# A decoder layer on one core: z transposed by VectorE in blocks through DRAM from batch 4 on, first loads on ScalarE's queue, first expert's inner weights in four loads

## The chip, the core and the metric

One core of a Trainium2 chip. Its engines run side by side and wait for each other by semaphores: PE (TensorE, matrix products; PEld is its loading of weights), DVE (VectorE), ACT (ScalarE), POOL (GpSimd) and SP (SyncE). Transfers between DRAM and SBUF are issued by SP and by ACT, each on its own queue, and run on 16 DMA engines. The metric is the device time of one execution in microseconds, as the median of several executions.

## What is computed

The layer takes x (16 batches of 512 tokens, 256 features), a context (16 x 64 x 256) and a mask. Cut to what matters:

```python
# 1. linear self-attention, K = 2, 16 heads of 16
q  = x + x @ Wq + bq
ks = x + x @ Wk[k] + bk[k];  vs = x + x @ Wv[k] + bv[k]      # both scaled by 1/sqrt(1024)
state = prod_k(ks_k^T @ vs_k)                                # per head 16 x 16
out = q @ state                                              # "z" in the kernel
out = layernorm(out) * ln_g + ln_b
x = layernorm(x + out @ Wo + bo)
# 2. cross-attention to the context, 16 heads of 64
sim = (x @ xWq.T) @ (context @ Wkv.T)_k^T * 64 ** -0.5;  masked softmax
x = layernorm(x + (attn @ v) @ Wout.T + b_out)
# 3. mixture of 8 experts, capacity 1024 of the 8192 tokens for each
w = softmax(x @ router_w.T + router_b)
y_e = relu(tokens_e @ experts_inter[e]) @ experts_out[e] * w
x = layernorm(x + scatter_add(y_e))
```

All in float32. With these inputs every token has a positive weight for every expert, so the first 1024 tokens (batches 0 and 1, the "head") are those that go through the experts.

## The kernel before

Tokens of a batch lie on 128 partitions, four tiles of 128 (`NT`), features along the row; two halves of 128 features (`NC`) make the contraction. A matmul needs its operand with features on partitions, so each activation that is multiplied is also made in a transposed copy: `xT` (for `ps_o`, L775), `zT` (for `ps_p`, L799), `x1T` (for `ps_sim`, L933). Eight more columns (`E`, hence `CX` = 264) carry the router's scores along with x, z and x1.

The work of a batch runs in streams, written as Python generators: `all_grams` (gram matrices of x, L634 to L651), `all_self_attention` (L697: `g_times_wk`, `states`, z in L775, its norm, `zT`, then `ps_p` in L799), `scores_operand` (L807: x1, its norm and `x1T`), `all_cross_attention` (L876: `ps_sim`, softmax, `ps_x` in L954), `all_routing` (L966) and `experts` (L1060: `ps_h` in L1077, `ps_e` in L1094, all on batches 0 and 1). `weave` (L1141) picks the next stream by a plan of start and span, and by a `Model` (L28) of each engine's and transfer's duration, which holds a stream back until what it waits for should be there (`until(made(...))`). `in_order` (L1161) then fixes the order that came out for PE, DVE, ACT (with its DMA issues) and POOL. SP's issues stand in the order that the tile framework gives them. So a number in `Model`, as the 5.0 us of a transfer on ACT's queue (L87), moves the order of instructions; it is no time of the chip.

There are two ways to a transposed copy. The helper `transposed` (L243) uses PE: eight transposes into two PSUM banks, copied out by ACT or DVE. From batch 4 (`FIRST`) on, `xT` and `x1T` go in blocks: `to_blocks` (L268) has DVE transpose 32 x 32 blocks into `xb` (one buffer, guarded by `taken`), `put_blocks` (L283) writes `xb` to DRAM on ACT's queue, and `from_blocks` (L291) reads it back in four transfers on ACT's queue, each to 32 partitions, which sets the blocks in place. This trip changes the order of the tokens: where a tile takes it, the tokens come out as (block, place in block) exchanged. So `x1T`'s trip needs x1 in one order and leaves another, and the gram's x of batches 4 on is loaded with its rows in the exchanged order (L364), for `xT` to come out in the natural one. z is transposed by PE in every batch (L788): eight transposes `ps_zt`, and two ACT activations that apply gain and shift while they copy out of PSUM (L789).

Setup: the first loads are all issued by SP, in this order: x of batch 0 in four pieces (L359), the first 512 rows of the context and of Wkv (L490, L500), the second ones, x of batch 1, the key weights (L388 on). ACT's first instruction is the load of its function table (L218). The x that self-attention adds to (`xt`, `load_x`, L692) is loaded when z's batch begins. The first expert's inner weights (`load_inter`, L1109, 1 MB in one transfer) can only be loaded once the setup's buffers are given back (`setup.close`, L975), which is after batch 0's last norm; `experts` waits in the model for them (L1069).

Of the kernel before, what the change touches and what calls it, by code (L numbers as in the profile page):

```python
# [9 lines left out]
FP = mybir.dt.float32  # L10
I32 = mybir.dt.int32
U8 = mybir.dt.uint8
AF = mybir.ActivationFunctionType
# [5 lines left out]
P = 128  # L19
# [8 lines left out]
class Model:  # L28
# [37 lines left out]
    def run(self):  # L66

        traced = self.nc.cur_bb.bb.instructions
        now = self.free.get("PE", 0.0)
        end = max(self.end, now)  # L70
        for ins in traced[self.seen:]:
            kind, engine = type(ins).__name__, str(ins.engine).split(".")[-1]
            aps = [[a.bass_ap for a in l if hasattr(a, "bass_ap")] for l in (ins.ins, ins.outs)]
            names = [[a.name for a in l] for l in aps]
            at = 0.0
            for made, used, l in ((1, 0, names[0]), (1, 1, names[1])):
                for n in l:
                    if kind == "InstDMACopy" and self.made.get(n, (0, 0))[1] == "SP":
                        continue
                    for known, book in ((made, self.made), (used, self.used)):  # L80
                        if known and n in book:
                            t, by = book[n]
                            at = max(at, t + (self.WIDE.get(by, 0.0) if by != engine else 0.0))
            if kind == "InstDMACopy" and engine == "Activation":
                start = max(at, self.free.get(engine, 0.0))
                self.free[engine] = start + 0.35
                done = start + 5.0  # L87
            elif kind == "InstDMACopy":
                size = 4 * min(a.size() for l in aps for a in l)
                if now < 40:  # L90
                    issue = self.free["SP"] = max(at, self.free.get("SP", 0.8)) + 0.45
                    self.dma = max(issue + 1.2, self.dma) + size / 300e3
                    done = self.dma + 0.4
                else:
                    done = at + size / 220e3 + 2.0
            elif names[1]:
                start = max(at, self.free.get(engine, 0.0))
                done = self.free[engine] = start + self.duration(ins, kind, engine)
                if engine == "PE":
                    self.took += done - start  # L100
                else:
                    end = max(end, done + 0.15)
            else:
                continue
            for n in names[0] + names[1]:
                by = "SP" if kind == "InstDMACopy" else engine
                self.used[n] = max(self.used.get(n, (0.0, None)), (done, by), key=lambda p: p[0])
            for n in names[1]:
                self.made[n] = (done, "SP" if kind == "InstDMACopy" else engine)
        self.seen, self.end = len(traced), end  # L110
        return end
# [13 lines left out]
def decoder_layer(  # L125
# [60 lines left out]
    def bank(name):  # L186
        return psp.tile([P, 512], FP, tag="ps", name=name)
# [26 lines left out]
        return t  # L214

    nc.scalar.preload_act_table_set("natural_log_exp_and_others")  # L218
    ident = const.tile([P, P], FP, tag="ident", name="ident")
    make_identity(nc, ident)  # L220
    eps = const.tile([P, 1], FP, tag="eps", name="eps")
# [107 lines left out]
    with ExitStack() as att:  # L329
# [19 lines left out]

        def load_gram_x(b, eng=nc.sync):  # L350


            t = gp.tile([P, NT, C + 1], FP, tag="gx", name="gx")
            nc.gpsimd.memset(t[:, :, C:], 1.0)
            pieces = 1 if 0 < b < FIRST else NT
            n_ = NT // pieces
            for i in range(pieces):
                if b < FIRST:
                    eng.dma_start(  # L359
                        out=t[:, i * n_:(i + 1) * n_, :C],  # L360
                        in_=x[b, i * n_ * P:(i + 1) * n_ * P, :].rearrange("(t p) c -> p t c", p=P),
                    )
                else:
                    eng.dma_start(  # L364
                        out=t[i * 32:(i + 1) * 32, :, :C],
                        in_=x[b, i * P:(i + 1) * P, :].rearrange("(q j) c -> j q c", j=32),
                    )
            return t

        gram_x = {0: load_gram_x(0)}  # L370
# [114 lines left out]

        BJ = B * J

        def load_context(sp, q):
            t = wk2.tile([P, 4, C], FP, tag="vo", name="cn", bufs=6)
            nc.sync.dma_start(  # L490
                out=t,
                in_=context.rearrange("b j c -> (b j) c")[q * 512:(q + 1) * 512, :].rearrange(
                    "(i p) c -> p i c", p=P
                ),
            )
            return t

        def load_wkv(sp, r4):
            t = wk2.tile([P, 4, C], FP, tag="vo", name="nat", bufs=6)
            nc.sync.dma_start(out=t, in_=x_wkv[r4 * 512:(r4 + 1) * 512, :].rearrange("(r p) c -> p r c", p=P))  # L500
            return t

        NG = 512 // (GB * J)
# [183 lines left out]
                    sums[b // QB][1].append(key_sums(sums["u4"]))  # L687
                    yield WAIT

        grams, sums, x_blocks = {}, {}, {}  # L690

        def load_x(b):  # L692
            t = wk1.tile([P, NT, CX], FP, tag="xt", name="xt")
            nc.sync.dma_start(out=t[:, :, :C], in_=x[b].rearrange("(t p) c -> p t c", p=P))
            return t

        def self_attention(b, done):  # L697
# [47 lines left out]
            nc.vector.scalar_tensor_tensor(state, state, STATE_SCALE, headmask, ALU.mult, ALU.mult)  # L745

            yield from until(lambda: finished["x1"] >= b)
            xt = load_x(b)
            if b < FIRST:
                yield from until(lambda: made(xt))  # L750
                transposed(xT.rearrange("p t c n -> p c t n"), xt, lambda t: t)
# [29 lines left out]
            yield from normalized(z[:, :, :C], lambda t: z[:, t, :C], mm=mm)  # L781
            yield WAIT

            zT = wk1.tile([P, NC, S], FP, tag="xT", name="zT")
            for cc in range(NC):
                ps = bank("ps_zt")
                for t in range(NT):
                    nc.tensor.transpose(ps[:, t * P:(t + 1) * P], z[:, t, cc * P:(cc + 1) * P], ident)  # L788
                nc.scalar.activation(  # L789
                    zT[:, cc, :], ps, AF.Identity, bias=cs["shift"][:, cc:cc + 1], scale=cs["gain"][:, cc:cc + 1]  # L790
                )
            nc.gpsimd.tensor_copy(xt[:, :, C:], z[:, :, C:])
            nc.gpsimd.tensor_add(xt[:, :, :C], xt[:, :, :C], cs["bo"].unsqueeze(1).to_broadcast([P, NT, C]))
            yield WAIT
            mm = moments()
            for t in range(NT):
                ps = bank("ps_p")
                for cc in range(NC):
                    nc.tensor.matmul(  # L799
                        ps[:, :CX], zT[:, cc, t * P:(t + 1) * P], wo[:, cc, :], start=(cc == 0), stop=(cc == NC - 1)  # L800
                    )
                nc.vector.tensor_add(xt[:, t, :], ps[:, :CX], xt[:, t, :])
                moment(mm, t, xt[:, t, :])
                yield
# [161 lines left out]
        def routing(b, x1):  # L966
# [5 lines left out]
            if b == 0:  # L972

                yield from until(lambda: ("values", 1) in held)
                setup.close()  # L975
                ffn = pool(att, "ffn", 1)
                first_expert.extend((load_inter(0), load_outer(0)))
            if b < HEAD_B:
                head_T[b] = ffn.tile([P, NC, S], FP, tag=f"head_T{b}", name="head_T", bufs=1)
                transposed(head_T[b], x2)  # L980
# [79 lines left out]
        def experts():  # L1060
# [5 lines left out]
            for e in range(E):  # L1066
                if e == 0:
                    wi, wo_ = first_expert
                    yield from until(lambda: made(wi, wo_))  # L1069
                for n in range(CAP // TB):  # L1070
                    b, t0 = divmod(n * TB // P, NT)
                    yield from until(lambda: b in head_T and made(head_T[b]))
# [33 lines left out]
                    if n == CAP // TB - 1 and e + 1 < E:  # L1106
                        wo_ = load_outer(e + 1)

        def load_inter(e):  # L1109
            t = ffn.tile([P, NC, FF], FP, tag="wi", name="wi", bufs=1)  # L1110
            nc.sync.dma_start(out=t, in_=w_inter[e].rearrange("(c p) f -> p c f", p=P))
            return t

        def load_outer(e):
# [66 lines left out]
        def until(ready):  # L1181
            while not ready():
                yield 0.5

        def all_grams():
            for b in range(B):
                if b >= QB:
                    grams_st.plan(SETUP + (b - QB - 0.8) * STEP, STEP, 2.9)
                yield from until(lambda: finished["states"] > b - 5)
                yield from grams_of([b])  # L1190
                if b == 1:
                    yield from until(lambda: made(early, wk, nbk))
                    finish_key_weights()
                    yield from router_columns(rw)
                    yield
                if b == QB - 1:
                    cs.update(rest_of_weights(sp))
                    yield
                    yield from until(lambda: made(early, wo, wv))
                    finish_weights()  # L1200
                    yield WAIT
                    yield from router_weights(sp)
# [33 lines left out]

        setup = ExitStack()
        sp = pool(setup, "setup", 2)
        nats = [load(sp, q) for q in range(2) for load in (load_context, load_wkv)]
        gram_x[1] = load_gram_x(1)  # L1240
        key_weights()
        cs = {}
# [101 lines left out]
```

## Time and profile before

| | us |
|---|---|
| median of 3 runs (1355.06 to 1358.25) | 1355.67 |
| the profiled execution | 1358.28 |
| its span, first to last instruction | 1356.3 |
| PE busy | 1334.3 |
| DVE, ACT, POOL busy | 817.4, 422.5, 204.2 |
| mean granted TensorE clock | 0.996 |
| DMA engines, mean | 132 GB/s |

How to read the profile lines. A line of the timeline has the start and the length in us, the engine (a q behind it marks the engine's sequencer, as for an issued DMA), the source line, the operation, output<-input by the kernel's names, shape, how many, and in brackets the idle time of the engine just before it with what ended it. A line of the groups has, behind the bar, the busy time in us and the mean length of one in ns, then the idle time before them. A line of the waits reads "who <- what released it: us in total, times, longest". A line of the stretches has from:to, its length, then the busy time and number of instructions of PE, PEld, DVE, ACT and POOL, the mean granted clock of TensorE (1.00 is full), the share of the DMA engines in use and GB/s. "issue" is a wait that the profile puts down to nothing it shows. Matmuls overlap: the length of one (some 0.27 to 0.6 us) is a latency, and the pace is the distance from one to the next.

### The profile page before, as it was taken

What the parts mean: (1) busy time and instruction counts of PE and PEld (TensorE: products, weight loads), DVE (VectorE), ACT (ScalarE), POOL (GpSimd) and SP (SyncE); (2) the same over time, 40 slices, a digit from 0 to 9 for tenths busy, and PEclk for the clock granted to TensorE, in tenths of its full rate; (3) what the DMA queues carried; (4) which work ended last, traced back from release to release, by engine and by line L of the source; (5) the groups of instructions that cost most, each with busy time, mean ns of one, the idle gap of its engine ahead of it and who ended that gap; (6) DMA issues with size and microseconds to landing.
All of it is one profiled execution on the core that took longest, in us unless ns stands there. A gap on an engine that the chain in (4) does not pass through costs nothing.

```text
span 1356.3 us, 23928 instructions
## 1 busy us (share of the span) xinstructions
PE 1334.3 (98%) x9438; PEld 1052.6 (78%) x9438; DVE 817.4 (60%) x1961; ACT 422.5 (31%) x970; POOL 204.2 (15%) x140
## 2 busy tenths in 40 slices
PE   8999998999999999999999999999999999999997
PEld 5676675887788787887788787877788787878796
DVE  1265837556474747567555758566655848474844
ACT  2244424242222514143222414142323304142323
POOL 0010201112021111202021111202111112112100
PEclk9999998999999999999999999999999999999999
DMA  8737474421535353723645353623635153605411
GB/s 264 210 128 241 159 225 157 118 74 41 151 119 150 110 152 96 205 70 112 172 128 142 95 154 124 185 64 110 182 88 155 63 160 109 176 30 126 129 56 41
DMA packets 115204, 178.73 MB, mean 132 GB/s; under 512 B 17032, under 2 KB 83856, under 8 KB 115088
## 3 DMA queue, kind: packets, MB, share of 16 engines
q1 hardware_dynamic: 97808, 151.98, 39.1%
q10 hardware_dynamic: 17280, 25.17, 5.5%
q8 instruction: 76, 1.25, 0.4%
q14 instruction: 40, 0.33, 0.1%
HBM read 127.29 MB, written 49.81 MB: 131 GB/s over the span
## 4 chain that ended last, share of the span: by engine, by line
PE 93%; DVE 4%; DMA 1%; issue 1%; ACT 1%; SPq 0%; POOL 0%; POOLq 0%; DVEq 0%; ACTq 0%
PE ps_x L954 17%; PE ps_h L1077 16%; PE ps_sim L933 15%; PE ps_e L1094 15%; PE ps_p L799 4%; PE ps_o L775 4%; PE ps_kv L511 4%; PE ps_gk L712 4%; PE ps_vo L571 2%; PE ps_kq L862 2%; PE ps_s L724 2%; PE ps_g L634 2%; PE ps_m L757 1%; PE ps_zt L788 1%; PE ps_g L639 1%; PE ps_t L249 1%
## 5 line engine op out<-in xcount | busy, mean ns | idle before, releaser
L1077 PE MATMUL ps_h<-head_T,wi 128*128 128x256 f32 x1024 | 243.4, 383 | 4.0 <-issue 4.0
L933 PE MATMUL ps_sim<-kq,x1T 128*128 128x512 f32 x512 | 237.8, 593 | 0.0
L1077 PEld LDWEIGHTS ps_h<-head_T,wi 128*128 128x128 f32 x1024 | 194.2, 192 | 49.8 <-issue 20.9
L954 PE MATMUL ps_x<-vo,pT 32*128 32x264 f32 x4096 | 232.5, 383 | 0.2 <-DVE off L321 0.2
L954 PEld LDWEIGHTS ps_x<-vo,pT 32*128 32x128 f32 x4096 | 209.5, 185 | 20.8 <-issue 2.3
L920 POOL TENSOR_TENSOR s<-s,sm 128x1024 f32<-128x1024 f32 x64 | 121.7, 1901 | 650.2 <-DVE sm L919 572.5
L961 DVE TENSOR_TENSOR x<-ps_x,x 128x264 f32<-128x264 f32 x64 | 23.2, 425 | 234.9 <-PE ps_x L954 234.9
L1083 ACT ACTIVATE hT<-ps_h 128x256 f32<-128x256 f32 x177 | 67.7, 382 | 302.3 <-PE ps_h L1077 266.8
L933 PEld LDWEIGHTS ps_sim<-kq,x1T 128*128 128x128 f32 x512 | 96.2, 190 | 77.7 <-issue 69.8
L939 DVE TENSOR_REDUCE mx<-ps_sim 128x8 f32<-128x512 f32 x128 | 86.2, 674 | 59.4 <-PE ps_sim L933 58.6
L911 ACT ACTIVATE s<-s 128x512 f32<-128x512 f32 x128 | 79.3, 624 | 88.9 <-DVE s L940 68.9
L940 DVE TENSOR_TENSOR s<-ps_sim,mx 128x512 f32<-128x512 f32 x128 | 88.5, 692 | 4.4
L922 DVE STREAM_TRANSPOSE pT<-s 128x1024 f32<-128x1024 f32 x64 | 78.5, 1226 | 4.5 <-POOL s L920 4.2
L918 DVE TENSOR_REDUCE sm<-s 128x16 f32<-128x1024 f32 x64 | 76.5, 1196 | 0.0
L324 ACT ACTIVATE x<-x,off,rstd 128x264 f32<-128x264 f32 (+1 forms) x112 | 58.4, 592 | 33.9 <-DVE off L321 29.5
L775 PE MATMUL ps_o<-m,xT 128*128 128x264 f32 x256 | 63.6, 389 | 0.0
L799 PE MATMUL ps_p<-wo,zT 128*128 128x264 f32 x256 | 62.0, 387 | 0.0
L799 PEld LDWEIGHTS ps_p<-wo,zT 128*128 128x128 f32 x256 | 48.5, 190 | 15.4 <-issue 6.6
L511 PE MATMUL ps_kv<-cT,wT 128*128 128x512 f32 x128 | 59.6, 596 | 0.3
L835 POOL TENSOR_TENSOR x<-x,bout 128x1056 f32<-128x1056 f32 x16 | 39.1, 2446 | 136.4 <-PE ps_t L249 43.2
L712 PE MATMUL ps_gk<-wk,g 128*128 128x256 f32 x256 | 59.4, 379 | 0.0
L712 PEld LDWEIGHTS ps_gk<-wk,g 128*128 128x128 f32 x256 | 48.5, 190 | 11.2 <-issue 4.9
(178 smaller groups left out, 1739.8 us busy)
## 6 DMA issues: line engine op xcount, KB each, us to landing
vo<-vo_dram SPq DMA_DIRECT2D x512, 132.0 KB, 4.1
vo_dram<-vst SPq DMA_DIRECT2D x64, 264.0 KB, 2.8
x_blocks<-xb ACTq DMA_DIRECT2D x24, 512.0 KB, 3.3
xt<-in_x_dram SPq DMA_DIRECT2D x16, 512.0 KB, 3.8
wi<-L_ffn_experts_inter_dram SPq DMA_DIRECT2D x8, 1024.0 KB, 4.8
x_rest<-x SPq DMA_DIRECT2D x14, 512.0 KB, 3.1
out_dram<-x SPq DMA_DIRECT2D x14, 512.0 KB, 4.5
gx<-in_x_dram SPq DMA_DIRECT2D x52, 128.0 KB, 3.8
```

The lines of the kernel that those rows point to most:

```text
L511: nc.tensor.matmul(ps, wT[:, cc, r % 4 * P:(r % 4 + 1) * P], cT[:, cc, q * 512:(q + 1) * 512], start=(cc == 0), stop=(cc == NC - 1),)
L712: nc.tensor.matmul(ps[:, :C], blk, wk[:, j, k, :], start=(j == 0), stop=(j == NC - 1))
L775: nc.tensor.matmul(ps[:, :CX], xT[:, t, cc], m[:, cc, :], start=(cc == 0), stop=(cc == NC - 1))
L799: nc.tensor.matmul(ps[:, :CX], zT[:, cc, t * P:(t + 1) * P], wo[:, cc, :], start=(cc == 0), stop=(cc == NC - 1))
L911: nc.scalar.activation(s[:, hs, :], s[:, hs, :], AF.Exp, scale=SCALE)
L920: nc.gpsimd.tensor_mul(s, s, sm.unsqueeze(2).to_broadcast([P, NH, J]))
L933: nc.tensor.matmul(ps, x1T[:, t, cc], kq[:, cc, hf * 512:(hf + 1) * 512], start=(cc == 0), stop=(cc == NC - 1),)
L939: nc.vector.tensor_reduce(mx[:, hs], sim, AX.X, ALU.max)
L940: nc.vector.tensor_sub(s[:, hs, :], sim, mx[:, hs].unsqueeze(2).to_broadcast([P, 8, J]))
L954: nc.tensor.matmul(ps[q][:, :CX], probsT[pq, blk].rearrange("p t i -> p (t i)"), vos[c][pq, i, :], start=(c == 0 and i == 0), stop=(c == 7 ...
L1077: nc.tensor.matmul(ps[:, :TB], wi[:, cc, f * P:(f + 1) * P], head_T[b][:, cc, t0 * P:t0 * P + TB], start=(cc == 0), stop=(cc == NC - 1),)
L1094: nc.tensor.matmul(ps[:, :C], hT[f][:, t * P:(t + 1) * P], wo_[:, f, :], start=(f == 0), stop=(f == NF - 1),)
```

## The change

1. z of batches 4 to 15 makes the trip in blocks: DVE transposes, ACT's queue writes and reads. ACT's gain and shift then run on `zT` in SBUF, in place. Since the trip exchanges the token order, the gram's x is now loaded in natural order in every batch (one transfer for each batch after 0), `xT` and z come out exchanged, and z's trip brings them back. The router's eight columns of z don't make that trip: SP writes them to DRAM (`z_columns`) and reads them back in four transfers with the order exchanged, into `xt`, in place of a POOL copy. `zT` has the layout of `xT`.
2. The first rows of the context and of Wkv are issued on ACT's queue, ahead of the load of its function table. Batch 0's `xt` is loaded in the setup (`first_x`).
3. The first expert's inner weights are loaded in four pieces of 256 columns, and `experts` doesn't wait in the model for them.
4. The model's time of a transfer on ACT's queue is 3.8 instead of 5.0 us.

```diff
             if kind == "InstDMACopy" and engine == "Activation":
                 start = max(at, self.free.get(engine, 0.0))
                 self.free[engine] = start + 0.35
-                done = start + 5.0
+                done = start + 3.8
...
-
-    nc.scalar.preload_act_table_set("natural_log_exp_and_others")
...
-            pieces = 1 if 0 < b < FIRST else NT
+            pieces = 1 if b > 0 else NT
             n_ = NT // pieces
             for i in range(pieces):
-                if b < FIRST:
-                    eng.dma_start(
-                        out=t[:, i * n_:(i + 1) * n_, :C],
-                        in_=x[b, i * n_ * P:(i + 1) * n_ * P, :].rearrange("(t p) c -> p t c", p=P),
-                    )
-                else:
-                    eng.dma_start(
-                        out=t[i * 32:(i + 1) * 32, :, :C],
-                        in_=x[b, i * P:(i + 1) * P, :].rearrange("(q j) c -> j q c", j=32),
-                    )
+                eng.dma_start(
+                    out=t[:, i * n_:(i + 1) * n_, :C],
+                    in_=x[b, i * n_ * P:(i + 1) * n_ * P, :].rearrange("(t p) c -> p t c", p=P),
+                )
...
-        def load_context(sp, q):
+        def load_context(sp, q, eng=nc.sync):
             t = wk2.tile([P, 4, C], FP, tag="vo", name="cn", bufs=6)
-            nc.sync.dma_start(
+            eng.dma_start(
...
-        def load_wkv(sp, r4):
+        def load_wkv(sp, r4, eng=nc.sync):
...
-            xt = load_x(b)
+            xt = first_x.pop() if b == 0 else load_x(b)
...
-            zT = wk1.tile([P, NC, S], FP, tag="xT", name="zT")
-            for cc in range(NC):
-                ps = bank("ps_zt")
+            zT = wk1.tile([P, NT, NC, P], FP, tag="xT", name="zT")
+            if b < FIRST:
+                for cc in range(NC):
+                    ps = bank("ps_zt")
+                    for t in range(NT):
+                        nc.tensor.transpose(ps[:, t * P:(t + 1) * P], z[:, t, cc * P:(cc + 1) * P], ident)
+                    nc.scalar.activation(
+                        zT[:, :, cc, :], ps.rearrange("p (t n) -> p t n", t=NT), AF.Identity,
+                        bias=cs["shift"][:, cc:cc + 1], scale=cs["gain"][:, cc:cc + 1],
+                    )
+                nc.gpsimd.tensor_copy(xt[:, :, C:], z[:, :, C:])
+                nc.gpsimd.tensor_add(xt[:, :, :C], xt[:, :, :C], cs["bo"].unsqueeze(1).to_broadcast([P, NT, C]))
+                yield WAIT
+            else:
+
+                zc = dram.tile([P, NT, E], FP, tag=f"z_columns{b}", name="z_columns")
+                nc.sync.dma_start(out=zc, in_=z[:, :, C:])
+                xb = yield from to_blocks(z)
+                there = put_blocks(f"z_blocks{b}", xb)
                 for t in range(NT):
-                    nc.tensor.transpose(ps[:, t * P:(t + 1) * P], z[:, t, cc * P:(cc + 1) * P], ident)
-                nc.scalar.activation(
-                    zT[:, cc, :], ps, AF.Identity, bias=cs["shift"][:, cc:cc + 1], scale=cs["gain"][:, cc:cc + 1]
-                )
-            nc.gpsimd.tensor_copy(xt[:, :, C:], z[:, :, C:])
-            nc.gpsimd.tensor_add(xt[:, :, :C], xt[:, :, :C], cs["bo"].unsqueeze(1).to_broadcast([P, NT, C]))
-            yield WAIT
+                    nc.sync.dma_start(
+                        out=xt[t * 32:(t + 1) * 32, :, C:], in_=zc[:, t, :].rearrange("(q j) e -> j q e", j=32)
+                    )
+                yield
+                yield from until(lambda: made(there, xt))
+                nc.gpsimd.tensor_add(xt[:, :, :C], xt[:, :, :C], cs["bo"].unsqueeze(1).to_broadcast([P, NT, C]))
+                from_blocks(zT, there)
+                yield
+                yield from until(lambda: made(zT))
+                for cc in range(NC):
+                    nc.scalar.activation(
+                        zT[:, :, cc, :], zT[:, :, cc, :], AF.Identity,
+                        bias=cs["shift"][:, cc:cc + 1], scale=cs["gain"][:, cc:cc + 1],
+                    )
+                yield WAIT
             mm = moments()
             for t in range(NT):
                 ps = bank("ps_p")
                 for cc in range(NC):
                     nc.tensor.matmul(
-                        ps[:, :CX], zT[:, cc, t * P:(t + 1) * P], wo[:, cc, :], start=(cc == 0), stop=(cc == NC - 1)
+                        ps[:, :CX], zT[:, t, cc], wo[:, cc, :], start=(cc == 0), stop=(cc == NC - 1)
                     )
...
-                first_expert.extend((load_inter(0), load_outer(0)))
+                first_expert.extend((load_inter(0, NF // 2), load_outer(0)))
...
                     wi, wo_ = first_expert
-                    yield from until(lambda: made(wi, wo_))
...
-        def load_inter(e):
+        def load_inter(e, pieces=1):
             t = ffn.tile([P, NC, FF], FP, tag="wi", name="wi", bufs=1)
-            nc.sync.dma_start(out=t, in_=w_inter[e].rearrange("(c p) f -> p c f", p=P))
+            n_ = FF // pieces
+            for i in range(pieces):
+                nc.sync.dma_start(
+                    out=t[:, :, i * n_:(i + 1) * n_],
+                    in_=w_inter[e, :, i * n_:(i + 1) * n_].rearrange("(c p) f -> p c f", p=P),
+                )
             return t
...
                     yield from until(lambda: made(early, wk, nbk))
+                    first_x.append(load_x(0))
                     finish_key_weights()
...
-        nats = [load(sp, q) for q in range(2) for load in (load_context, load_wkv)]
+        nats = [load(sp, q, (nc.scalar, nc.sync)[q]) for q in range(2) for load in (load_context, load_wkv)]
+
+        nc.scalar.preload_act_table_set("natural_log_exp_and_others")
```

More of the change, by code (lines that the diff above doesn't have):

```diff
@@ L496, in load_context @@
             return t
-        def load_wkv(sp, r4):
+        def load_wkv(sp, r4, eng=nc.sync):
             t = wk2.tile([P, 4, C], FP, tag="vo", name="nat", bufs=6)
-            nc.sync.dma_start(out=t, in_=x_wkv[r4 * 512:(r4 + 1) * 512, :].rearrange("(r p) c -> p r c", p=P))
+            eng.dma_start(out=t, in_=x_wkv[r4 * 512:(r4 + 1) * 512, :].rearrange("(r p) c -> p r c", p=P))
             return t
@@ L688, in grams_of @@
                     yield WAIT
-        grams, sums, x_blocks = {}, {}, {}
+        grams, sums, x_blocks, first_x = {}, {}, {}, []
         def load_x(b):
```

## The prediction

> **What bounds the kernel now.** I read the page's busy shares first, then who waits for whom on PE, then the stretches and the order of time around each PE pause, and last the group of the transposes that the change removes.
>
> ```profile
> PE 1334.3 (98%) x9438; PEld 1052.6 (78%) x9438; DVE 817.4 (60%) x1961; ACT 422.5 (31%) x970; POOL 204.2 (15%) x140
> ```
> ```profile
> PE ps_h L1077 <- issue: 4.0, 1, 4.0
> PE ps_g L634 <- DMA gx<-in_x_dram: 2.9, 1, 2.9
> PE ps_m L757 <- DVE state L745: 2.4, 2, 1.2
> PE ps_t L249 <- DMA cn<-in_ctx_dram: 1.8, 1, 1.8
> PE ps_t L249 <- ACT x L324: 1.5, 4, 1.0
> PE ps_t L249 <- DMA xt<-in_x_dram: 1.4, 1, 1.4
> ```
> PE is idle for 22.0 of 1356.3 us: 6.9 after its last matmul, 2.9 before the first, the rest in the rows above. So time falls only if PE gets less to do or one of these rows shrinks; DVE, ACT and DMA cost time only where PE comes to wait for them.
>
> ```profile
> 214.62 0.38 SPq L1111 DMA_DIRECT2D wi<-L_ffn_experts_inter_dram  x1
> 219.68 6.48 PE L1077 MATMUL ps_h<-head_T,wi 128*128 128x256 f32 x16 [4.05 <-issue]
> ```
> ```profile
> 215.50:219.70 4.20, 0.15 (x3) 0.06 (x1) 4.15 (x6) 0.84 (x2) 1.31 (x1) 0.86 0.84 314
> 219.70:225.30 5.60, 5.60 (x13) 4.49 (x14) 2.64 (x8) 0.88 (x3) 1.54 (x4) 0.50 0.40 141
> ```
> The largest pause is the first expert's. PE stops at 215.63, wi (1 MB) lands 4.8 us after its issue, and the granted clock (the 0.50) halves from 218.5 to 225.3: 16 matmuls take 6.48 us, where the same 16 at 1152.00 take 3.45.
>
> ```profile
> L788 PE MATMUL ps_zt<-ident,z 128*128 128x128 f32 x128 | 17.1, 275 | 0.1
> L789 ACT ACTIVATE zT<-ps_zt,shift,gain 128x512 f32<-128x512 f32 x32 | 23.0, 770 | 43.8 <-PE ps_zt L788 43.8
> L274 DVE STREAM_TRANSPOSE xb<-x 128x256 f32<-128x256 f32 x48 | 20.0, 426 | 0.0
> ```
> ```profile
> 298.97 1.04 PE L788 MATMUL ps_zt<-ident,z 128*128 128x128 f32 x8
> 299.84 1.89 PE L1094 MATMUL ps_e<-wo__1985,hT 128*128 128x256 f32 x8
> ```
> The 275 ns are one transpose's latency. What eight occupy on PE is the distance to the next group, 299.84 - 298.97 = 0.87 us.
>
> **The change, part by part.**
>
> *z's transposes.* The built program has 96 PE transposes fewer (12 batches of 8) and, up to batch 3, PE's order is as before but for one group. Gain 12 x 0.87 = **10.4**. Added on DVE: 48 x 0.43 = 20.6 us, on an engine that is idle 40%; it is hidden by PE's other streams (experts, cross attention), and would cost at most its 20.6 if every one stood in PE's way. On ACT: 12 puts of 0.35 and 48 reads of 0.44 to issue, 25 us, and 24 activations that read SBUF instead of PSUM (nearest row L911, also 128x512 from SBUF, 624 ns) for 24 of 770. ACT is busy 31%. POOL loses 12 copies of 0.21.
>
> The skill speaks against this part: the Trainium skill, VectorE: DVE Perf Modes, section Rules for kernel authors, sends a 128x128 transpose to TensorE whenever PSUM is a fitting target. By that rule nothing is to be won; by the row above, 10.4 us, because here TensorE is the engine without idle time. No run here yet shows which holds.
>
> The new chain is long, and whether PE meets it is the question. From the last ps_o to a normalized z the twelve batches take 5.5 (397.2 to 402.7 in batch 4) to 12.4 us. x1 already makes the same trip (four transposes, a put, four reads): from its first transpose to the last landing 12.2 to 19.6 us over the twelve, 15.5 in batch 4 (428.9 to 444.4). Two activations add 1.3. So z's chain takes 19.0 to 33.3 us, typically 25. In the changed program's PE order, with each group at its pace before, the work between a batch's last ps_o and its first ps_p is 29.6 to 46.4 us (before, 13.9 to 24.0): other work covers the typical chain everywhere, the longest one not where the cover is 29.6. x1's own trip, from the last ps_p to the landing, took 22.5 to 34.5 us; its cover is now 24 to 60, and in batches 7, 11, 12 and 15 it stands within 1.5 us of what that batch took before. I set **+3** for pauses: four of some 0.7. Ends: -4.4 (the pauses behind L745, 2.4, and in the 260 to 340 stretch, 2.0, happen not to recur) and 12 x 3.7 = +44 (every chain 33.3 against 29.6).
>
> Queues: a batch adds to SP one write of z's eight router columns and four reads that wait for it, and its x load has three issues fewer. Rows near them are the mask load (16 KB, 3.3 us) and nbk (1 KB in four-byte pieces, 5.7): about 3.3 + 4 x 0.45 + 3.3 = 8 us, beside a blocks trip of at least 12; without that cover it would lengthen the chain by its own 8 to 13. SP stands still for some 3 us; behind it lie the next vo and x loads, wanted 30 us later. On ACT the reads wait for the put; queued behind are experts' relus and exponentials. Before, ACT stood 41.0 us in five such waits (longest 20.7) and PE's list of waits has no row for it.
>
> *First expert.* Four pieces of 256 KB on SP, whose first two blocks need only the first. Its landing is bounded by the 128 KB reads (2.4 at best) and 1 MB (4.8); I take the 256 KB row, k_dram, 2.9: PE starts at 217.5 instead of 219.68, **-2.1**. [...] A pause of 1.9 us should leave the clock whole: it fell 2.9 us after PE stopped, and stayed at 1.00 through the 1.83 us pause at 6.7. That saves half of 5.6, **-2.8**. Ends: 0 and -6.9.
>
> *Start.*
> ```profile
> 2.69 0.43 SPq L490 DMA_DIRECT2D cn<-in_ctx_dram  x1
> 8.55 1.06 PE L249 MATMUL ps_t<-ident,cn 128*128 128x128 f32 x8 [1.83 <-DMA cn<-in_ctx_dram]
> 59.39 1.06 PE L249 MATMUL ps_t<-ident,xt 128*128 128x128 f32 x8 [1.35 <-DMA xt<-in_x_dram]
> ```
> On ACT's queue cn is issued near 0.82 instead of 2.69, and lands 1.9 us earlier, as PE ends its first group (6.72): the 1.83 go. But PE's order now puts batch 1's ps_g ahead of the first ps_kv, near 9.5; gx of batch 1 is issued 1.0 earlier than before (4.81) and takes 5.5 to land, so 9.3 to 10.3. I take **-1.3** (0 to -1.8). The table load on ACT (1.28 us) moves behind the two issues, and ACT's first copy is at 9.21. Loading batch 0's xt ahead removes the 1.35: **-1.3**; it lands in a stretch where DMA is 0.87 busy, and what it pushes back, wv, is issued 24.7 us ahead of its use at 46.8.
>
> Sum: -10.4 -2.1 -2.8 -1.3 -1.3 +3.0 = -14.9. The profiled execution took 1358.28 (span 1356.3 and 2.0 around it), 2.6 above the median 1355.67. So 1343.4 for such an execution, and **1341** against the median.
>
> **Rivals.** Below, 0.3% (4 us) is what counts as no change, about what a measurement can tell.
>
> A. The forecast, 1341, own range 1333 (no pauses: -17.9, first expert's pause gone whole, -2.0, and two old ones, -2.4) to 1350 (12 us of pauses instead of 3). Chance 0.64.
>
> B. The freed PE time turns into waits for ACT and for zT, about 1.3 us a batch, 15 us: 1355.7 - 17.9 + 15 = 1353. For it: batches 7, 11, 12, 15, and reads of up to 7.8 us instead of 2.8. Against: no row of x1T or xT in PE's waits before. Chance 0.20; a third of it within 4 us of before.
>
> C. Slower: z's round trip becomes the wait of every batch at ps_p. It decides from 17.9/12 = 1.5 us a batch; at the worst sum (3.7) it is 1355.7 - 17.9 + 44 = 1382, more if pauses beyond 2.9 us halve the clock again. For it: ACT carries two round trips a batch, each read waiting for its put, in one queue with the evacuations of PE's banks. Against: the cover of 30 to 46 us. Chance 0.13.
>
> D. The change doesn't do what it says in its small parts: the first piece queues with the other three and lands at 4.8, the clock halves again, and gx of batch 1 gives back the start: -10.4 -1.3 +3 = 1347. Chance 0.03.
>
> Faster by over 0.3%: A, D and two thirds of B, 0.80; within: 0.07; slower: 0.13. The range is 1333 to 1356, with C left out.
>
> **What will show it.** Right: ps_zt x32 instead of x128; no wait above 0.5 us at ps_p or ps_sim; the first ps_h waiting under 2.5 us with clock 1.00 after it; no pause before cn and xt. Wrong: rows "PE ps_p <- ACT zT" or "ps_sim <- DMA x1T" of several us in sum, ACT's waits for z_blocks behind them, a second stretch of clock 0.50, or, at the start, a wait for gx of batch 1 above 1 us.

## The result, and the profile after

| | before | after |
|---|---|---|
| median, us | 1355.61 (6 runs, 1355.06 to 1358.36) | 1361.62 (6 runs, 1360.18 to 1364.41) |
| ratio, 95% interval | | 1.0039 [1.0028, 1.0051] |
| profiled execution, its span | 1358.28, 1356.3 | 1364.41, 1362.7 |

The changed kernel is slower, by 5 to 6 us, where 14.9 less were forecast. First the page's busy times and three groups of instructions of the changed kernel:

```profile
PE 1336.3 (98%) x9342; PEld 1049.6 (77%) x9342; DVE 830.2 (61%) x2025; ACT 419.6 (31%) x954; POOL 201.7 (15%) x128
```
```profile
L780 PE MATMUL ps_zt<-ident,z 128*128 128x128 f32 x32 | 4.4, 275 | 0.1
...
L272 DVE STREAM_TRANSPOSE xb<-z 128x256 f32<-128x256 f32 x48 | 19.9, 426 | 5.5 <-DMA x_blocks<-xb 5.5
...
L272 DVE STREAM_TRANSPOSE xb<-x 128x256 f32<-128x256 f32 x48 | 19.2, 420 | 22.6 <-DMA x_blocks<-xb 22.6
```

The 96 transposes are gone from PE; counted from the start of each matmul to the start of the next, `ps_zt` takes 3.80 us instead of 14.66. DVE's 48 transposes of z take what was forecast. New is the last column: DVE stands still for 22.6 us ahead of x1's transposes and 5.5 ahead of z's, until an earlier write out of `xb` has ended. Before, this column was 0.0. What PE waits for in the changed kernel (total, times, longest):

```profile
PE ps_g L625 <- DMA gx<-in_x_dram: 5.0, 3, 3.7
PE ps_x L969 <- DVE pT L937: 3.4, 2, 3.2
PE ps_m L748 <- DVE state L736: 2.8, 3, 1.0
PE ps_h L1091 <- issue: 2.0, 1, 2.0
PE ps_t L247 <- ACT x L322: 1.5, 4, 1.0
PE ps_kq L877 <- DVE hT L1099: 1.2, 1, 1.2
PE ps_kq L877 <- DVE kq L885: 1.1, 2, 0.6
PE ps_x L969 <- DMA vo<-vo_dram: 0.8, 2, 0.6
PE ps_sim L948 <- DMA x1T<-x_blocks: 0.8, 1, 0.8
...
PE ps_p L814 <- ACT zT L805: 0.4, 1, 0.4
```

The first expert's 4.0 has become 2.0, and the waits for `cn` and `xt` are gone. But the first x is waited for three times instead of once (5.0 against 2.9), and `pT`, `kq`, `hT`, all made by DVE, are new. The two places that the forecast watched, `ps_p` and `ps_sim`, hold 0.4 and 0.8; the second is above the 0.5 that it named as its sign. The longest new pause, in order of time (changed kernel, timeline, then three stretches with the granted clock behind the five engines):

```profile
804.32 1.90 POOL L935 TENSOR_TENSOR s<-s,sm 128x1024 f32<-128x1024 f32 x1 [5.68 <-DVE sm L934]
...
805.21 0.34 ACTq L283 DMA_DIRECT2D x_blocks<-xb  x1
...
806.73 3.72 PE L766 MATMUL ps_o<-m,xT 128*128 128x264 f32 x16
...
810.29 1.90 PE L625 MATMUL ps_g<-gx 128*128 128x257 f32 x8
813.72 0.45 DVE L272 STREAM_TRANSPOSE xb<-x 128x256 f32<-128x256 f32 x1 [7.23 <-DMA x_blocks<-xb]
814.09 1.20 DVE L937 STREAM_TRANSPOSE pT<-s 128x1024 f32<-128x1024 f32 x1
```
```profile
811.50:814.90 3.40, 0.69 (x4) 0.26 (x2) 1.18 (x2) 0.00 (x0) 0.00 (x0) 1.00 0.08 28
814.90:818.30 3.40, 2.95 (x27) 2.95 (x31) 3.23 (x10) 0.00 (x0) 0.00 (x0) 0.50 0.00 0
818.30:821.70 3.40, 3.40 (x67) 3.40 (x64) 1.86 (x7) 0.49 (x1) 1.35 (x1) 0.99 0.09 12
```

The write of gx's blocks is issued at 805.21 and has landed 8.4 us later, the longest of the kernel's writes. x1's first transpose needs the same `xb`, stands at the head of DVE's queue for 7.23 us, and behind it stands `pT`, whose input is ready at 806.22 (POOL's scaling, 1.90 us from 804.32). PE runs out of work at 812.19 and goes on at 815.35, at half clock for 3.4 us.

### The profile page after: what moved, and what is told of

Same layout as the page of the kernel before. It is cut to its first block, busy times and chain, and to the rows that moved or that the text cites. A ratio compares the mean times of both kernels' runs of the same rounds, so it can differ in the third digit from the quotient of the medians.

```text
span 1362.7 us, 23971 instructions
## 1 busy us (share of the span) xinstructions
PE 1336.3 (98%) x9342; PEld 1049.6 (77%) x9342; DVE 830.2 (61%) x2025; ACT 419.6 (31%) x954; POOL 201.7 (15%) x128
## 3 DMA queue, kind: packets, MB, share of 16 engines
q8 instruction: 76, 1.25, 0.4%
## 4 chain that ended last, share of the span: by engine, by line
PE 85%; DVE 7%; DMA 6%; ACT 1%; issue 1%; SPq 1%; ACTq 0%; DVEq 0%
PE ps_x L969 15%; PE ps_sim L948 15%; PE ps_e L1108 14%; PE ps_h L1091 14%; PE ps_kv L502 4%; PE ps_p L814 4%; PE ps_gk L703 4%; PE ps_o L766 3%; PE ps_vo L562 2%; PE ps_s L715 2%; PE ps_g L625 2%; PE ps_kq L877 2%; DMA vo<-vo_dram 2%; DMA x_blocks<-xb 2%; PE ps_m L748 1%; PE ps_g L630 1%
## 5 line engine op out<-in xcount | busy, mean ns | idle before, releaser
L969 PE MATMUL ps_x<-vo,pT 32*128 32x264 f32 x4096 | 239.5, 385 | 4.4 <-DVE pT L937 3.4
L1091 PE MATMUL ps_h<-head_T,wi 128*128 128x256 f32 x1024 | 237.8, 382 | 2.3 <-issue 2.0
L969 PEld LDWEIGHTS ps_x<-vo,pT 32*128 32x128 f32 x4096 | 214.6, 186 | 27.0 <-DVE pT L937 5.1
L948 PE MATMUL ps_sim<-kq,x1T 128*128 128x512 f32 x512 | 230.7, 593 | 0.8 <-DMA x1T<-x_blocks 0.8
L1097 ACT ACTIVATE hT<-ps_h 128x256 f32<-128x256 f32 x164 | 62.7, 383 | 271.4 <-PE ps_h L1091 271.2
L315 ACT ACTIVATE rstd<-bn_mv,eps 128x4 f32<-128x4 f32 (+1 forms) x70 | 20.7, 296 | 186.1 <-DVE bn_mv L303 112.3
```

The lines of the kernel that those rows point to most:

```text
L948: nc.tensor.matmul(ps, x1T[:, t, cc], kq[:, cc, hf * 512:(hf + 1) * 512], start=(cc == 0), stop=(cc == NC - 1),)
L969: nc.tensor.matmul(ps[q][:, :CX], probsT[pq, blk].rearrange("p t i -> p (t i)"), vos[c][pq, i, :], start=(c == 0 and i == 0), stop=(c == 7 ...
L1091: nc.tensor.matmul(ps[:, :TB], wi[:, cc, f * P:(f + 1) * P], head_T[b][:, cc, t0 * P:t0 * P + TB], start=(cc == 0), stop=(cc == NC - 1),)
```

## The experiments

"Order kept" means that PE, DVE, ACT and POOL carry out their instructions in the order of the kernel that is edited, because the model is told the old names and durations. Ratios are to the kernel before, with their 95% interval; 0.001 is 1.36 us.

**The parts alone (e1 to e4), each on the kernel before.**

e1, the start:

```diff
-        nats = [load(sp, q) for q in range(2) for load in (load_context, load_wkv)]
+        nats = [load(sp, q, (nc.scalar, nc.sync)[q]) for q in range(2) for load in (load_context, load_wkv)]
+        nc.scalar.preload_act_table_set("natural_log_exp_and_others")
...
-            xt = load_x(b)
+            xt = first_x.pop() if b == 0 else load_x(b)
```

> The kernel before with the start's edits alone: the first context and Wkv rows on ACT's queue, the table load behind them, batch 0's xt loaded ahead. Theory 1 (the start gains nothing: in the changed kernel the first x landed 0.8 us later, two more waits stand between x's pieces, and the full clock came at 12.8 instead of 6.9 us): ratio 1.000 to 1.003, 0 to 4 us longer, xt's 1.35 us already counted. Rival, as predicted: both small waits go and nothing replaces them, 2.6 us shorter, ratio 0.998.

Measured: 1357.69 us, 1.0009 [1.0001, 1.0018], as theory 1 has it. On the timeline of e1 the second and third pieces of x come late too:

```profile
3.66 1.20 PE L633 MATMUL ps_g<-gx 128*128 128x257 f32 x2 [3.66 <-DMA gx<-in_x_dram]
5.30 1.23 PE L633 MATMUL ps_g<-gx 128*128 128x257 f32 x2 [0.45 <-DMA gx<-in_x_dram]
7.27 2.08 PE L633 MATMUL ps_g<-gx 128*128 128x257 f32 x4 [0.74 <-DMA gx<-in_x_dram]
```

They were issued as before; what is new is that two loads of 512 KB run beside them. Full clock comes at 12.8 us (before: 6.9).

e2, the first expert:

```diff
-                first_expert.extend((load_inter(0), load_outer(0)))
+                first_expert.extend((load_inter(0, NF // 2), load_outer(0)))
...
-                    yield from until(lambda: made(wi, wo_))
```

> The kernel before with the first expert's edit alone: four loads of 256 KB, no wait in the model. As predicted, and as the changed kernel's trace has it (pause 1.96 us, clock 1.00 behind it): 4 to 5.5 us shorter, ratio 0.996 to 0.997. Rival: the gain was given back at a later wait, 0 to 2 us shorter.

Measured: 1351.33 us, 0.9970 [0.9959, 0.9980]: as predicted. The pause is 1.92 us and the clock stays at 1.00.

e3, z's trip (the `else` branch of the diff, `load_gram_x` with it), 5.0 us kept:

> The kernel before with z's transposes in blocks via DRAM alone (gx in one piece and natural rows with it), the model's 5.0 us kept. Theory 1 (the trip itself: DVE's added work and the longer chain make PE meet state, pT, kq and vo late, which eats the 10.9 us that the transposes left): 2 to 8 us longer, ratio 1.002 to 1.006. Rival 2 (the order made with 3.8 us is what places the late operands, the trip alone is sound): 5 to 10 us shorter, ratio 0.993 to 0.996.

Measured: 1386.43 us, 1.0217 [1.0204, 1.0230], far outside both. PE's waits in e3 show a new place:

```profile
PE ps_tot L1039 <- DVE ranks L1035: 11.3, 1, 11.3
```

In this order the experts' blocks are used up 2 us after batch 15's last `ps_x`; its norm and routing then run with PE idle, and the last 28 us are at half clock. The rest is late operands, as after the full change.

e4, the model's number alone:

```diff
-                done = start + 5.0
+                done = start + 3.8
```

> The kernel before with the model's 3.8 us instead of 5.0 alone: nothing but the order of instructions changes, from the first batch with block transposes on. Theory 1: within 1.5 us of before. Rival 2 (the order): 2 to 8 us longer, with pauses at ps_x, ps_kq or ps_m that the kernel before has not.

Measured: 1362.69 us, 1.0048 [1.0035, 1.0061], as rival 2 has it: with no work changed, an order alone costs 6.5 us. The timeline of e4 shows how:

```profile
486.06 1.90 POOL L920 TENSOR_TENSOR s<-s,sm 128x1024 f32<-128x1024 f32 x1 [3.48 <-DVE sm L919]
...
486.63 1.61 DVE L744 TENSOR_TENSOR state<-sk 128x256 f32<-128x256 f32 x1
487.92 2.59 POOL L835 TENSOR_TENSOR x<-x,bout 128x1056 f32<-128x1056 f32 x1
488.27 2.52 DVE L745 SCALAR_TENSOR_TENSOR state<-state,headmask 128x256 f32<-128x256 f32 x1
490.71 1.23 DVE L922 STREAM_TRANSPOSE pT<-s 128x1024 f32<-128x1024 f32 x1
490.84 1.34 PE L757 MATMUL ps_m<-state,wqT 128*128 128x128 f32 x8 [2.07 <-DVE state L745]
```

The two operations on `state` have all their sources in SBUF. Alone they take 0.42 us; here each ends 0.28 us after POOL's operation, and PE waits 2.07 us.

**Do the parts add up? (e5 to e8)** e5 is e3 with 3.8; e6 the changed kernel without its z branch and with gx loaded as before; e7 the changed kernel with 5.0; e8 is e2 with the `first_x` lines of e1.

> The kernel before with z's block transposes and the model's 3.8 us together (the changed kernel without its start and first-expert edits). If parts add up: the changed kernel's +6.0 less the start's +1.3 and the first expert's -4.7 leaves +9, 1365, ratio 1.007. Rival (the order is made anew by every edit, so pauses do not add up): outside 1361 to 1369.

Measured: 1362.87 us, 1.0045 [1.0032, 1.0059].

> The changed kernel with z's transposes on TensorE again (gx as before), all other edits kept, 3.8 us in the model. If parts add up: +1.3 -4.7 +6.6 = +3.2, 1359, ratio 1.0024. If z's trip is the loss of the changed kernel and the order is not: 1350 to 1353, ratio 0.997.

Measured: 1359.94 us, 1.0023 [1.0014, 1.0031].

> The changed kernel with 5.0 us in the model again. If parts add up: e3's +30 and +1.3 -4.7 make 1382, ratio 1.020, with PE out of work before the router's totals at the end, as in e3 (11.3 us of pause, then half clock). Rival (e3's end was an accident of one order): below 1370.

Measured: 1383.06 us, 1.0193 [1.0179, 1.0207], with the same 11.3 us at `ps_tot`.

> The kernel before with the first expert's four loads and batch 0's xt loaded ahead, nothing on ACT's queue, z on TensorE, 5.0 us. Expected: e2's 4.7 and 1.2 of xt's pause, 1350, ratio 0.9955 to 0.9965. Rival (the earlier xt load delays weights that PE waits for, as the start's edits together gained nothing): 1351.5 to 1353.

Measured: 1352.27 us, 0.9969 [0.9957, 0.9980].

The start and the first expert together, -2.9 by e1 and e2, add up with e3 (-3.3, e7) and e4 (-3.4, e6), less clearly with e5 (-0.8, uncertain by 2.4). z's trip and the model's number do not add up: the trip costs 29.4 us in the order that 5.0 makes (e3), and nothing more in the order that 3.8 makes (e4 1.0048, e5 1.0045). In neither order are the 10.9 us that leave PE to be seen in the time. e8's pause at `xt` is gone from the trace, but against e2 no gain is measured.

**The new wait and the stretched operation (e9 to e12), orders kept.** e10 to e13 leave work out, so they show what it costs and are no kernels to use. e9 writes z's and x1's blocks into the tile that they will be read back into, which is free at that time:

```diff
...
-        xb = wk1.tile([P, NT, NC, NT, 32], FP, tag="xb", name="xb")
+        if place is None:
+            xb = wk1.tile([P, NT, NC, NT, 32], FP, tag="xb", name="xb")
+        else:
+            xb = place.rearrange("p t c (q j) -> p t c q j", j=32)
+            model.tile(place.name + "_xb", (id(wk1.pool), "xb"), wk1.bufs)
...
-                xb = yield from to_blocks(z)
+                xb = yield from to_blocks(z, zT)
...
-                xb = yield from to_blocks(x1)
+                xb = yield from to_blocks(x1, x1T)
```

> The changed kernel, the order of PE, DVE, ACT and POOL kept instruction for instruction; only z's and x1's blocks are written into the buffer of their own target (zT, x1T), so that the one buffer xb serves gx alone. Theory (the third user of xb is the loss: DVE stands 31.0 us in eight waits for xb's put, pT is queued behind one of 7.2, PE waits 3.16 and the clock halves for 3.4): those waits below 2 us in sum, the pause at 812 and the half clock behind it gone, 5 to 8 us shorter than the changed kernel, 1354 to 1357, ratio 0.999 to 1.001. Rival (the operands are late for other reasons, ACT's waits above all): less than 1.5 us shorter, ratio 1.003 or more.

Measured: 1355.32 us, 0.9991 [0.9982, 0.9999], 6.3 us less than the changed kernel. The groups and the same spot on the timeline of e9:

```profile
L283 DVE STREAM_TRANSPOSE zT<-z 128x256 f32<-128x256 f32 x48 | 19.8, 426 | 0.7 <-DMA xt<-z_columns 0.2 <-issue 0.2 <-DMA x_rest<-x 0.2
L283 DVE STREAM_TRANSPOSE x1T<-x 128x256 f32<-128x256 f32 x48 | 19.2, 418 | 0.0
```
```profile
803.25 0.34 ACTq L296 DMA_DIRECT2D x_blocks<-xb  x1
804.45 0.43 DVE L283 STREAM_TRANSPOSE x1T<-x 128x256 f32<-128x256 f32 x1
804.81 1.20 DVE L953 STREAM_TRANSPOSE pT<-s 128x1024 f32<-128x1024 f32 x1
```

x1's transpose no longer waits for the write of 803.25, `pT` follows at once, and the pause with its half clock is gone. This is the largest single cause that was found in the changed kernel.

e10 takes POOL's add of bout out of the changed kernel, all but 9 columns, with its planned duration kept:

```diff
-            nc.gpsimd.tensor_add(x1, x1, cs["bout"].unsqueeze(1).to_broadcast([P, NT, CX]))
+            nc.gpsimd.tensor_add(x1[:, :, :9], x1[:, :, :9], cs["bout"][:, :9].unsqueeze(1).to_broadcast([P, NT, 9]))
```

> The changed kernel, order kept, with POOL's add of bout on 9 of the 264 columns (left out on the others; 2.5 us of POOL become some 0.2). Theory (DVE's operations with two sources in SBUF stretch from 0.42 to 2.0 us beside this add, and so state comes late to ps_m three times): the pauses at ps_m, 2.8 us in sum, gone or below 0.3 each, 2.5 to 4.5 us shorter than the changed kernel, ratio 1.000 to 1.002. Rival (state is late for what stands ahead of it on DVE): pauses unchanged, ratio 1.0035 or more.

Measured: 1362.31 us, 1.0048 [1.0035, 1.0061]: no gain, pauses unchanged. But the rival's reason isn't right either; the timeline of e10 names another partner, the scaling of the probabilities:

```profile
499.28 1.90 POOL L936 TENSOR_TENSOR s<-s,sm 128x1024 f32<-128x1024 f32 x1 [1.01 <-DVE sm L935]
499.42 2.04 DVE L737 SCALAR_TENSOR_TENSOR state<-state,headmask 128x256 f32<-128x256 f32 x1
```

> e9 and e10 together. If both theories hold and add up: 1350.5 to 1354, ratio 0.996 to 0.9985. Rival (a pause that goes comes back later in another place): no shorter than the better of the two by 1 us.

Measured: 1355.21 us, 0.9992 [0.9983, 1.0001]: e9's gain alone.

> e4 (the kernel before in the order that 3.8 us make), order kept, with POOL's add of bout on 9 of 264 columns. Theory: e4's two pauses at ps_m (2.07 and 2.70) and the two half clocks of 3.4 us behind them (1.7 us each) are DVE's stretched operations: 7 to 8.5 us shorter than e4, 1354 to 1356, ratio 0.999 to 1.000. Rival (the order itself is worse): 1360 or more, ratio 1.003 or more.

Measured: 1356.15 us, 1.0000 [0.9991, 1.0009]: e4's whole loss is gone, with its order unchanged. On the timeline of e12 `state<-state,headmask` starts at 489.88, takes 0.43, and `ps_m` does not wait. So the order is not bad by itself; it lets two operations of DVE meet POOL's add.

**What is left in e9 (e13 to e16).** e13 is e9 with POOL's scaling cut short:

```diff
-                nc.gpsimd.tensor_mul(s, s, sm.unsqueeze(2).to_broadcast([P, NH, J]))
+                nc.gpsimd.tensor_mul(s[:, :, :1], s[:, :, :1], sm.unsqueeze(2))
```

> e9 (own buffers), order kept, with POOL's scaling of the probabilities on 16 of 1024 elements a partition (the others stay unscaled). Theory (DVE's state operation, 2.04 us instead of 0.42 beside it, is what PE waits for at ps_m at 500, 576 and 1167): these three pauses gone, 2.5 to 4 us shorter than e9, ratio 0.996 to 0.9975. Rival (state is late for what stands ahead of it on DVE): pauses stay, within 1 us of e9.

Measured: 1349.86 us, 0.9956 [0.9941, 0.9971], 5.5 less than e9 by the medians (4.7 by the ratios), order kept. The three pauses at `ps_m`, 2.8 us in sum, are gone. More than expected went with them: a pause at `ps_kq` fell from 1.25 to 0.79 us and the half clock at 1202 behind it is gone. e13 also hands `pT` its input 1.7 us sooner; what that alone is worth was not separated. The group of `state` in e9, in e13, then in the kernel before:

```profile
L749 DVE SCALAR_TENSOR_TENSOR state<-state,headmask 128x256 f32<-128x256 f32 x16 | 10.0, 627 | 0.6
```
```profile
L750 DVE SCALAR_TENSOR_TENSOR state<-state,headmask 128x256 f32<-128x256 f32 x16 | 6.8, 425 | 0.6
```
```profile
L745 DVE SCALAR_TENSOR_TENSOR state<-state,headmask 128x256 f32<-128x256 f32 x16 | 10.5, 657 | 0.6
```

The mean of 627 ns is 425 with some of 2.04 us among them: a mean far above the shortest form of the same shape is the sign of such a meeting. So the kernel before has such meetings too, and its two pauses at `ps_m`, 2.4 us in sum, stand behind them (2.52 us beside the add of bout at 790.73, 2.04 beside the scaling at 1091.14).

e14, e9 with the first loads on SP:

> e9 with the first context and Wkv rows on SP again and the table load first (xt still ahead). The order differs in one ps_g group. Theory (the loads on ACT's queue hold up x's first pieces by 0.7 to 1.9 us and the full clock by some 3): 2 to 3 us shorter than e9, 1352.5 to 1353.5, ratio 0.997 to 0.998. Rival (the start is neutral): within 1 us of e9.

Measured: 1355.24 us, 0.9992 [0.9981, 1.0003]: no gain, the expectation missed. In its profiled execution the first x came 0.8 us sooner, but the first expert's pause, 1.94 us, was followed by half clock, which e9's 1.84 was not.

e15 lets the model know the buffers and the meeting, and plans anew; its rule for the meeting:

```diff
+                if engine == "Pool":
+                    self.port = start, start + self.duration(ins, kind, engine)
+                elif engine == "DVE" and len(aps[0]) > 1 and not any(n.startswith(("ps_", "ks_")) for n in names[0]):
+                    if self.port[0] <= start < self.port[1]:
+                        start = self.port[1]
```

> z's and x1's blocks in their targets' buffers as in e9, SP's start as in e14, and a model that knows both: no wait for xb there, and DVE's operations with two sources in SBUF wait for a running POOL operation. All of the order is made anew, with 3.8 us. Theory (the order is the rest: with a true model the pauses at ps_m and ps_kq go): 1344 to 1350, ratio 0.991 to 0.996. Rival (each new order meets other late operands, whatever these two rules say): 1351 to 1362.

Measured: 1368.22 us, 1.0074 [1.0050, 1.0099]. PE now waits 8.8 us for x1T's transfers (longest 4.6). The rival's direction, and beyond its range (1351 to 1362): this order made anew meets other late operands.

> e8 (z on TensorE, first expert's four loads, xt ahead, 5.0 us) with the model's rule for DVE beside POOL; order made anew. Theory: the two pauses at ps_m (1.2 each) go, 1348 to 1350, ratio 0.994 to 0.9955. Rival: new pauses elsewhere, 1352 to 1360.

Measured: 1352.32 us, 0.9968 [0.9955, 0.9981]: one pause of 1.6 at `ps_m` and one of 1.5 at `ps_x`; no better than e8.

**The scaling on DVE (e17, e18).** The edit of e9 and of e8, planned as if POOL still did it:

```diff
-                nc.gpsimd.tensor_mul(s, s, sm.unsqueeze(2).to_broadcast([P, NH, J]))
+                nc.vector.tensor_mul(s, s, sm.unsqueeze(2).to_broadcast([P, NH, J]))
```

> e9 (own buffers) with the scaling of the probabilities on DVE instead of POOL, at the same place of the order; PE's and ACT's orders kept. Theory (the meeting of the engines is the cost; 64 x 1.1 = 70 us more on DVE, busy 62%, are covered): state never stretched, 2 to 5 us shorter than e9, 1350 to 1353, ratio 0.996 to 0.998. Rival (the 1.1 us stand ahead of state, pT and kq on DVE and make them as late as POOL did): 1355 or more, ratio 0.999 or more.

Measured: 1384.68 us, 1.0212 [1.0196, 1.0228].

> e8 (z on TensorE, first expert's four loads, xt ahead) with the scaling on DVE in the same way. Theory: the two pauses at ps_m, 1.2 us each, and what they cost around go, 2 to 3.5 us shorter than e8, 1348 to 1350, ratio 0.994 to 0.9955. Rival: 1351 or more.

Measured: 1384.09 us, 1.0207 [1.0192, 1.0222]. The rival was right both times. The first two of PE's waits in e17, then in e18:

```profile
PE ps_m L763 <- DVE state L751: 9.3, 6, 2.8
PE ps_x L988 <- DVE pT L956: 5.7, 6, 2.7
```
```profile
PE ps_x L957 <- DVE pT L925: 14.2, 8, 3.2
PE ps_m L759 <- DVE state L747: 7.4, 4, 3.3
```

DVE was busy 62% in e9 and 61% in e8, yet the scaling, 1.24 and 1.30 us in each of 64 places on DVE, makes the kernels 29 and 32 us longer. These two waits were 2.8 us together in e9 and 2.4 in e8; they are 15.0 and 21.6 now. What counts there is how long an operand stands in DVE's queue just then, not DVE's share.

Of the kernels that compute everything, e2, e8 and e16 are the best and beat both (0.997).

## Why the prediction was wrong

- *z's transposes, -10.4.* Right on PE: -10.9. The Trainium skill, VectorE: DVE Perf Modes, section Rules for kernel authors, which the prediction set aside, would send these transposes to TensorE. With the one `xb` the runs side with it: e6 1.0023, the changed kernel 1.0039. With the blocks in their targets' buffers they don't: e9, with the same start, first expert and 3.8 as e6, though in another order, has 0.9991. With 5.0 in the model the kernels with z on TensorE are the best (e8); own buffers with 5.0 were not tried.
- *First expert, -4.9.* Right: e2 measured -4.1 (0.9970; by the medians -4.7). The 2.8 us of it for the clock were in part luck: the changed kernel's pause of 1.96 us kept full clock, e14's of 1.94 did not. A slip without weight: the 3.45 us at full clock are a distance to the next group, where the 6.48 are a length; as a length they are 3.62.
- *Start and xt, -2.6.* Wrong by some 4: e1 measured +1.2. The 1.83 us at `cn` came from one profiled execution; the traces of e2, e4 and e8, whose first loads are on SP as before, have no such wait. And the cost to x's own pieces was left out: only the second batch's gx was weighed, and that by the median of its group (5.5). In the trace before it is issued at 4.81 and lands 9.4 us later; in e1 it is issued at 4.89, not 1.0 earlier, and lands 6.9 later.
- *New pauses, +3.* The step that failed. The measured 5.3 (1.0039) less the other terms (-10.9, -4.1, +1.2) leaves +19. The prediction compared the length of z's trip with PE's other work up to `ps_p` and `ps_sim`, and there it was nearly right (0.4 and 0.8 us). It called DVE's added 20.6 us "hidden by PE's other streams" and did not ask what an added transpose waits for, nor what stands behind it on DVE: the one `xb` has three users a batch instead of two, and `pT` stands behind. That costs 6.3 (e9). The meeting of `state` with POOL is no large part of the +19, though e13 gains 5.5 without the scaling: PE's waits at `ps_m` are 2.8 us in the changed kernel and were 2.4 before. The remaining 13 or so weren't undone by an experiment, and their cause stays open. From start to start, the traces of e9 and of the kernel before put 5.1 of them at `ps_kq`, whose 512 matmuls occupy PE for 35.3 us in e9 and 30.2 before (and in e8), 2.8 at `ps_x` (234.1 and 231.3), and 1.7 at the half clock at 1202, right behind a pause at `ps_kq`. `ps_kq` takes so long only with both edits: 30.7 with the trip alone (e3), 31.2 with the 3.8 alone (e4), 34.6 with both (e5). One of its stages on the timeline of e8, then of e9:

```profile
742.11 3.84 PE L862 MATMUL ps_kq<-kT,xwq 64*128 64x128 f32 x64
...
743.30 2.05 ACT L872 COPY kq<-ps_kq 128x512 f32<-128x512 f32 x4 [1.55 <-PE ps_kq L862]
```
```profile
758.61 3.17 PE L893 MATMUL ps_kq<-kT,xwq 64*128 64x128 f32 x50
...
759.41 2.06 ACT L335 ACTIVATE z<-z,off,rstd 128x256 f32<-128x256 f32 x4
...
761.38 2.00 ACT L903 COPY kq<-ps_kq 128x512 f32<-128x512 f32 x4
...
762.33 1.16 PE L893 MATMUL ps_kq<-kT,xwq 64*128 64x128 f32 x14 [0.56 <-DVE kq L901]
```

  In e9 ACT's copies out of PSUM start 2.8 us after the first matmul instead of 1.2, behind the norm of z. That this makes `ps_kq` longer is read from the trace and was not tried.
- *The model's number.* The prediction took the new order into account as a list of PE's groups, "with each group at its pace before", and gave no price to which operations of other engines meet. e4 and e12 show that price: 6.5 us in the kernel before. In the changed kernel's order it is not POOL's add that costs (e10).
- *Rival C* had the sign and the wrong place: z's trip did not become a wait at `ps_p`; it held up the engine that does the transposes.

## What to carry to other kernels

When work is moved to an engine that is half idle, list for each moved instruction which buffer it must wait for and what stands behind it in that engine's queue; where a single buffer gets one more user, try the target's own memory first. Where a planner fixes the order, measure its constant alone: an unchanged program in another order was 6.5 us slower here, as much as the whole change.

## What the runs showed of the hardware

- An operation of DVE with both sources in SBUF that starts during one of POOL's lasts until that one ends: `state<-state,headmask` 0.42 us alone, 2.04 beside the scaling, 2.52 beside the add of bout. In the traces of all 20 kernels the two operations on `state` start 86 times during POOL's scaling or full add, and each time end 0.28 to 0.32 us after it. `pT`'s transpose, with one source, took 1.20 to 1.25 us alone (42 in the kernel before) and 1.19 to 1.25 beside one of POOL's operations on two tensors (22). The Trainium skill, SBUF — State Buffer, section Who interferes with whom, says it: such an instruction contends with a GpSimd instruction that reads SBUF, and the later one blocks fully. These traces agree.
- The clock is decided in windows of 3.413 us that run on from the start to the end of a program: in e4 the half clocks, 3.41 us each, begin at 218.61, 491.68 and 1095.84, 80 and 177 such windows apart. Over the traces of all 20 kernels (7816 windows at full clock, 37 of them followed by half clock), a window at full clock was followed by half clock in every case with more than 2.0 us of PE idle in it, and in none with less than 1.8, save windows with much `ps_x` or `ps_kq` (32 and 64 rows, down to 0.81 us) and one in e15. So a pause of 1.9 us costs 1.7 more (half of a window), or nothing, by where it falls: e14's 1.94 us lie in one window, the changed kernel's 1.96 at 218.63 in two. The Trainium skill, TensorE: Matmul & The Clock Gate, states the window in What's actually happening, and warns of gaps above about 3 us in Why this matters for your kernels; here 2.0 us in one window were enough.
